# Graph layer on one core: row places read from SBUF as byte offsets, and two queues that each fetch a tile of every fourth group

## The chip, the cores and the metric

The kernel runs on one core of a Trainium2 chip. The metric is device microseconds (us) of one execution; the number quoted for a kernel is the median of several executions. Engines are called as the profile calls them: PE is TensorE (PEld its weight load), DVE is VectorE, ACT is ScalarE, POOL is GpSimd, SP is SyncE. A name with q behind it (ACTq, SPq) is the sequencer of that engine, which also issues DMAs.

## The reference

One pre-normalised graph layer over N = 12500 nodes with D = 256 features and E = 200000 edges, sorted by `dst`; H = 512.

```python
h = maximum(layernorm(x), 0)
agg = segment_sum(h[src], dst, num_segments=N)
z = (1 + eps_gin) * h + agg
t = relu(batchnorm(dot(z, W1) + b1, g1, bt1))
out = relu(batchnorm(dot(t, W2) + b2 + h, g2, bt2))
return x + out
```

The expensive part is `segment_sum(h[src], dst)`: 200000 rows have to be fetched from DRAM in the order of `src`, and rows with the same `dst` are added.

## The kernel before

**Tiles and groups.** 128 edges make a tile, 12 tiles (GT) a group; there are 1563 tiles (NTILE) and 131 groups (NG). For each tile the 128 rows named by `src` are brought into SBUF, one row to a partition. PE then multiplies them with a 0/1 matrix (`oh`, made by DVE at L600) that says which edge belongs to which of the next 128 nodes; all tiles of a group add up in one PSUM tile `ps` (L636). The group's sum is copied out (`zs`, L691 on DVE), moved to its place among the nodes by a second 0/1 matrix (`at`, L700; `pz`, L708), and added to `zc`, which holds 512 nodes at a time (L723). When all groups of a chunk of 512 nodes are in, PE multiplies it with W1 in four slices (`ph`, L733); DVE takes the slice's statistics (`st`, L744), ACT copies it to `ts` (L750) and stores it in DRAM (`t_tab`, L751). A group spans some 96 nodes, so a chunk has 5 1/3 groups and there are 0.75 slices to a group. `ph` has three PSUM buffers, `ts` four.

**Two halves of the edges.** For the first 30 groups (LEAD) the rows come from `x` itself and are normalised after they have arrived, while the normalised table `h_tab` (rows of 512 numbers, 2048 bytes: the value and its rounding rest) is still being written. From group 30 on, the rows come from `h_tab`.

**Who fetches the rows.** Nearly every tile is fetched by POOL with one indirect DMA of 128 rows (`gather`, L567), whose row numbers lie in SBUF (`srcT`). The table `SINGLES` (L31) takes single tiles away from POOL: tile 0 of the groups 34, 40, 46, ... is fetched by SP, tile 0 of the groups 37, 43, 49, ... by ACT, 15 tiles each. Such a tile is fetched row by row (`fetch`, L534 to L549): a piece is 32 rows; the engine loads the piece's 32 node numbers into registers (L541: first the address of `src` is loaded, then an offset added to it, then the 32 numbers loaded from DRAM), and then for each row multiplies the number by the row's size (an instruction that the trace calls FUSED_REGOPS) and issues one DMA of 2048 bytes (L546, after a MOVE). The four pieces of a tile are issued in steps of their own, from seven steps (SOONER) before the tile's group is added up to three steps before. The rows go to the twelve row places in `gta` and `gtb`, which the first 30 groups used before; each place has a semaphore, for which PE waits ahead of that tile's matmul. Tile 0 is the last one that PE takes in a group.

**Order of the work.** The program is written out by hand: each engine's instructions stand in the order of the Python loop over steps i, one step to a group. In step i POOL's gathers of group i + 4 (AHEAD) stand first, then the work of DVE and ACT (ACT: the copies `ts` with their stores, and now and then a scaling of `zc`, L593), then PE's sums of group i with the second matmul of group i - 3 and one slice of W1 between them, and last on SP the load of the next chunk of `zc` (L589) and on SP and ACT the pieces that are due. So on ACT a piece stands behind the copies of its step and ahead of those of the next.

**After the groups** (from about 1933 us) the chunks of `t` are read back, normalised, multiplied with W2, normalised again and added to `x`. The change does not touch this.

Of the kernel before, what the change touches and what calls it, by code (L numbers as in the profile page):

```python
# [7 lines left out]

F32 = mybir.dt.float32
F32R = mybir.dt.float32r  # L10
I32 = mybir.dt.int32
AF = mybir.ActivationFunctionType
OP = mybir.AluOpType
# [3 lines left out]
P = 128  # L17
R = 4
EPS = 1e-5
GT = 12  # L20
# [7 lines left out]
XIN = 1  # L28
PIECE = 32
SOONER = 7  # L30
SINGLES = (("sync", 34, 6), ("scalar", 37, 6))  # L31


COPIES = 2
# [6 lines left out]
def kernel(  # L41
# [16 lines left out]
    nc = tc.nc  # L58
    N, D = x.shape
# [29 lines left out]
    h_tab = dram.tile([N, 2 * D], F32, name="h_tab")  # L89
# [72 lines left out]
    at = 0  # L162
# [6 lines left out]
    with ExitStack() as es:  # L169
# [20 lines left out]
        at = 0  # L190
# [48 lines left out]
        place = raw.tile([P, NG], I32, name="place")  # L239
# [3 lines left out]
        for i in range(EARLY):  # L243
            for t in reversed(range(GT)):
                k = i * GT + t
# [21 lines left out]
        for k, (v, t0, rows, n, e) in enumerate(checks):  # L267
# [7 lines left out]
                op0=OP.add, op1=OP.max,  # L275
# [76 lines left out]
    def fast():  # L352

        parts = []
        for n0, w in chunks:
            n = w * R
# [20 lines left out]
        with ExitStack() as fs:  # L377
# [14 lines left out]
            with ExitStack() as es:  # L392
                rows_pool = es.enter_context(tc.tile_pool(name="rows", bufs=RING))
                sel = es.enter_context(tc.tile_pool(name="sel", bufs=2))
                zcp = es.enter_context(tc.tile_pool(name="zc", bufs=4))
                tsp = es.enter_context(tc.tile_pool(name="ts", bufs=4))
                ps_i = es.enter_context(tc.tile_pool(name="ps_i", bufs=1, space=PSUM))
# [82 lines left out]
                def h_chunk(g):  # L480
# [3 lines left out]
                    relus(((0, R, xts.pop(g)),), n, ((0, R, hts[g]),), "c", g)  # L484
                    nc.scalar.copy(both_place[:, :n, 0, :].bitcast(F32R), hts[g][:, :n, :])
                    x_chunk(g + 3)
# [34 lines left out]
                alone, due = {}, {}  # L521
                for name, i0, every in SINGLES:
                    for i in range(i0, NG - 8, every):
                        alone.setdefault(i, []).append((name, every))
                arrived = [tc.alloc_semaphore(f"arrived{k}") for k in range(len(singles_at))]
                placing = {}
                for i in sorted(alone):
# [6 lines left out]
                def fetch(name, step):  # L534

                    eng = getattr(nc, name)
                    for i, j, q in due.pop((name, step), ()):
                        k, _ = placing[i, j]
                        place, c = singles_at[k]
                        e0 = (i * GT + j) * P + q  # L540
                        _, ids = nc.values_load_multi_w_load_instructions(  # L541
                            src[e0 : e0 + PIECE].rearrange("(o e) -> o e", o=1), engines=[eng.engine],
                            min_val=0, max_val=N - 1, skip_runtime_bounds_check_because="src names nodes",
                        )
                        for r, node in enumerate(ids):
                            single = eng.dma_start(place[q + r : q + r + 1, c, :], h_tab[bass.ds(node, 1), :])  # L546
                            tc.no_tile_sem_insts.add(single.ins.name)
                            tc.add_to_no_dep_group(f"single{i}_{j}", single.ins)
                            single.then_inc(arrived[k], 16)  # L549
# [34 lines left out]
                zc, ohs, summed, zss, ats, placed, slices = {}, {}, {}, {}, {}, {}, {}  # L584
# [10 lines left out]
                def edges(i):  # L595
# [4 lines left out]
                    nc.vector.tensor_tensor(  # L600
                        oh.bitcast(F32R) if i >= LEAD else oh,
                        col[:, :P].unsqueeze(1).to_broadcast([P, n, P]),
# [186 lines left out]
                for c in range(NCH):  # L789
                    k = min(max(first(c) - 2, c + 2), NG - CLOSE - 1)  # L790
# [154 lines left out]
            with tc.tile_pool(name="ps_y", bufs=2, space=PSUM, reuse_waits="tile") as ps_y:  # L945
# [117 lines left out]
                for p in range(1, PAIRS - 1):  # L1063
                    a, b = 2 * p, 2 * p + 1
# [47 lines left out]
                a, b = 2 * p, 2 * p + 1  # L1112
# [45 lines left out]
            with tc.tile_pool(name="ps_o", bufs=4, space=PSUM, reuse_waits="tile") as ps_o:  # L1158
# [18 lines left out]
                for k, g in enumerate(order):  # L1177
# [15 lines left out]
                    for c0, c1, rows in pieces(g):  # L1193
                        if c0 == c1:
                            continue
                        if k == 0:
                            nc.vector.scalar_tensor_tensor(
                                xt[:rows, c0:c1, :], po[:rows, c0:c1, :], 0.0, xt[:rows, c0:c1, :],
                                op0=OP.max, op1=OP.add,
# [255 lines left out]
```

## Time and profile before

| what | value |
|---|---|
| median of 3 runs | 2136.57 us (2135.61 to 2137.64) |
| the profiled execution, its own time | 2139.61 us |
| span of its trace | 2137.7 us |
| POOL busy in the span | 1539.0 us, 72% |
| PE busy | 1470.1 us, 69% |
| DVE busy | 880.4 us, 41% |
| ACT busy | 490.3 us, 23% |
| time of the DMA packets, as a share of 16 engines' span | POOL's queue 56.6%, SP's 17.9%, ACT's 3.9% |

The busy times count what an engine computes; loading registers, register arithmetic and the issuing of DMAs do not count, so ACT with 23% can be occupied far more than that. In a line of groups stand the line of the program, the engine, the operation, the tiles, how many there are, the busy time, the mean of one in ns, and the idle time of the engine just ahead of them with what ended it; "issue" there means that the engine's own sequencer was the last to be ready.

### The profile page before, as it was taken

The page shows a single profiled execution, that of the slowest core. Times are in us where ns is not written, and L with a number is a line of the kernel's source. Part 1 is how long each engine was busy: PE and PEld are TensorE (multiplying, and loading weights), DVE is VectorE, ACT ScalarE, POOL GpSimd, SP SyncE. Part 2 cuts the span into 40 slices and gives each one's busy share as a digit, 9 for nine tenths or more (in the row PEclk, how much of TensorE's full clock was granted, in tenths as well). Part 3 has the DMA queues.
Part 4 walks back from the last instruction along what each step waited for, and adds up shares of the span by engine and source line. Part 5 has one row for each costly group of instructions (what it writes and reads, how often), then busy time and mean ns, then how long its engine had stood idle before and what let it go on. Part 6 is the DMA issues. An engine that isn't in the chain of part 4 may idle for free.

```text
span 2137.7 us, 25061 instructions
## 1 busy us (share of the span) xinstructions
PE 1470.1 (69%) x3698; PEld 822.5 (38%) x3698; DVE 880.4 (41%) x1296; ACT 490.3 (23%) x873; POOL 1539.0 (72%) x1579
## 2 busy tenths in 40 slices
PE   2656657675667776666666666766776666679997
PEld 2545445453333333333333333333333333335445
DVE  6666676653222232222223223223222222136997
ACT  4766677750000000000000000000000000004555
POOL 7777777777777777777777777777777777774640
PEclk9778888888776676766677677767677767679999
DMA  6777777658888778787877787877778787878888
GB/s 186 245 244 247 258 236 266 225 163 243 243 237 241 232 241 239 229 246 237 241 232 238 240 241 231 239 239 239 233 236 244 227 237 231 265 235 275 308 308 342
DMA packets 189893, 520.52 MB, mean 243 GB/s; under 512 B 34056, under 2 KB 49328, under 8 KB 189718
## 3 DMA queue, kind: packets, MB, share of 16 engines
q0 software_dynamic: 111088, 354.65, 56.6%
q1 hardware_dynamic: 59842, 134.01, 17.9%
q10 hardware_dynamic: 18788, 30.17, 3.9%
q14 instruction: 144, 1.18, 0.2%
q8 instruction: 31, 0.51, 0.1%
HBM read 441.90 MB, written 76.80 MB: 243 GB/s over the span
## 4 chain that ended last, share of the span: by engine, by line
POOL 46%; issue 19%; DMA 15%; PE 11%; DVE 5%; ACT 3%; SPq 0%; ACTq 0%; DVEq 0%; POOLq 0%
POOL gt L567 45%; DMA gt<-h_tab,srcT 7%; DMA gt<-in_x_dram,srcT 4%; DMA gta<-in_x_dram,srcT 3%; PE one L994 2%; PE ps L636 2%; PE pr L994 2%; PE pq L994 2%; PE ph L733 1%; DVE stc L434 1%; ACT gt L458 1%; DVE stg L434 1%; DVE zc L723 1%; DVE gt L512 1%; PE pz L708 1%
## 5 line engine op out<-in xcount | busy, mean ns | idle before, releaser
L567 POOL DMA_INDIRECT gt<-h_tab,srcT x1173 | 1108.8, 945 | 357.6 <-issue 345.4
L636 PE MATMUL ps<-gt,oh 128*128 128x512 f32 (+1 forms) x1590 | 821.4, 597 | 457.1 <-DMA gt<-h_tab,srcT 433.6
L636 PEld LDWEIGHTS ps<-gt,oh 128*128 128x128 f32 x1590 | 382.2, 241 | 873.3 <-DMA gt<-h_tab,srcT 685.3
L744 DVE BATCH_NORM_STATS2 st<-ph 128x6 f32<-128x512 f32 x96 | 66.8, 696 | 689.3 <-PE ph L733 689.3
L600 DVE TENSOR_TENSOR oh<-col,dstT 128x1536 fp32r<-128x1536 f32 (+1 forms) x129 | 226.3, 1755 | 240.6 <-PE ps L636 240.3
L750 ACT COPY ts<-ph 128x512 f32<-128x512 f32 x96 | 56.1, 584 | 1069.7 <-issue 760.6
L733 PE MATMUL ph<-zc,w1s 128*128 128x512 f32 (+1 forms) x392 | 260.8, 805 | 55.7 <-DVE gt L512 55.7
L567 POOL DMA_INDIRECT gt<-in_x_dram,srcT x216 | 212.3, 983 | 67.2 <-issue 28.3
L708 PE MATMUL pz<-at,zs 128*128 128x256 f32 x516 | 201.6, 533 | 17.8 <-DVE zc L723 10.9
L708 PEld LDWEIGHTS pz<-at,zs 128*128 128x128 f32 x516 | 141.9, 277 | 47.7 <-issue 10.9
L733 PEld LDWEIGHTS ph<-zc,w1s 128*128 128x128 f32 x392 | 103.1, 267 | 140.8 <-issue 74.7
L723 DVE TENSOR_TENSOR zc<-pz,zc 128x512 f32<-128x512 f32 (+7 forms) x185 | 90.8, 516 | 108.9 <-PE pz L708 108.9
L458 ACT ACTIVATE gt<-gt,nbg,rsg 128x256 f32<-128x256 f32 x216 | 108.1, 588 | 11.8 <-DVE nbg L452 11.8
L434 DVE BATCH_NORM_STATS2 stg<-gt 128x6 f32<-128x512 f32 x108 | 72.8, 695 | 88.3 <-DMA gt<-in_x_dram,srcT 88.1
L567 POOL DMA_INDIRECT gta<-in_x_dram,srcT x80 | 79.8, 997 | 24.4 <-issue 7.0
L500 PE MATMUL ph<-ident,gt 128*128 128x128 f32 x196 | 36.5, 332 | 87.1 <-DVE gt L512 70.2
L593 ACT ACTIVATE zc<-zc,gin 128x1024 f32<-128x1024 f32 (+1 forms) x25 | 28.2, 1128 | 291.4 <-issue 268.6
L691 DVE TENSOR_REDUCE zs<-ps 128x256 f32<-128x512 f32 x99 | 67.2, 679 | 19.0 <-PE ps L636 19.0
L636 PE MATMUL ps<-gta,oh 128*128 128x256 f32 (+1 forms) x232 | 69.6, 438 | 0.0
L500 PEld LDWEIGHTS ph<-ident,gt 128*128 128x128 f32 x196 | 27.0, 168 | 96.9 <-DVE gt L512 53.9
L1015 POOL TENSOR_TENSOR ax<-ax,by 128x1024 f32<-128x1024 f32 x10 | 25.4, 2536 | 51.0 <-ACT by L972 46.8
L700 DVE TENSOR_SCALAR at<-col,shift 128x256 f32<-128x256 f32 x129 | 61.1, 474 | 2.3 <-PE pz L708 2.3
(189 smaller groups left out, 1224.8 us busy)
## 6 DMA issues: line engine op xcount, KB each, us to landing
h_tab<-gt SPq DMA_DIRECT2D x24, 1024.0 KB
t_tab<-ts ACTq DMA_DIRECT2D x96, 256.0 KB
gta<-h_tab SPq DMA_DIRECT2D x1280, 2.0 KB
gta<-h_tab ACTq DMA_DIRECT2D x1280, 2.0 KB
gt<-h_tab,srcT POOLq DMA_INDIRECT x1173, 4.4
gt<-in_x_dram SPq DMA_DIRECT2D x24, 512.0 KB
h_cols<-gt SPq DMA_DIRECT2D x24, 512.0 KB
zc<-h_cols SPq DMA_DIRECT2D x24, 512.0 KB
```

What stands on the lines that cost most here:

```text
L434: nc.vector.bn_stats(st[:, c : c + 2, :].rearrange("p c s -> p (c s)"), two.rearrange("p c d -> p d c"),)
L458: nc.scalar.activation(slot(to, c), slot(v, c), AF.Relu, bias=nb[:, c : c + 1], scale=rs[:, c : c + 1])
L500: nc.tensor.transpose(ph[:, c * P : (c + 1) * P], ht[:, c, d * P : (d + 1) * P], ident)
L567: nc.gpsimd.indirect_dma_start(out=slot(ga, t - t0)[:rows], out_offset=None, in_=x if i < LEAD else h_tab, in_offset=bass.IndirectOffsetOn ...
L600: nc.vector.tensor_tensor(oh.bitcast(F32R) if i >= LEAD else oh, col[:, :P].unsqueeze(1).to_broadcast([P, n, P]), dstT[:, t0 : t0 + n].uns ...
L636: part = nc.tensor.matmul(to, lhsT=lhsT, rhs=rhs, start=(j == order[0]), stop=(j == order[-1]))
L691: nc.vector.tensor_reduce(zss[i], ps.rearrange("p k d -> p d k"), axis=mybir.AxisListType.X, op=OP.add)
L708: nc.tensor.matmul(pz[:, d, :n], lhsT=zs[:, d * P : (d + 1) * P], rhs=at[:, :n], start=True, stop=True)
L723: nc.vector.tensor_add(side, pz[:, :, a - lo : b - lo], side)
L733: nc.tensor.matmul(ph[:, :n], lhsT=w1s[:, d, f * P : (f + 1) * P], rhs=zc[c][:, d, :n], start=(d == 0), stop=(d == DC - 1),)
L744: nc.vector.bn_stats(st1[:, f, c, :], ph[:, :n])
L994: nc.tensor.matmul(ps, lhsT=w[:, k, :], rhs=t[:, k, :], start=(k == 0), stop=(k == DC - 1))
```

## The change

Three things change. The node numbers of the tiles in SINGLES are loaded once, near the start, into two small SBUF tiles (`nodes`, a row of 128 for each tile) by two DMAs on SP, and DVE multiplies each by the row's 2048 bytes (`starts`, one instruction for SP's tiles, one for ACT's). `fetch` loads its 32 registers from a row of `starts` instead of from DRAM. Since `h_tab` and the row place are named as bytes (`bitcast(U8)`), the register is the byte offset itself, and the multiplication for each row is gone from the program. And SINGLES now takes tile 0 of the groups 34, 38, ..., 122 for SP (23 tiles) and of the groups 36, 40, ..., 120 for ACT (22 tiles): 45 tiles instead of 30. A tile's four pieces now fall into four steps in a row, so that SP has one piece in each step from 27 to 118, and ACT one in each from 29 to 116.

```diff
--- before.py
+++ after.py
@@ -8,6 +8,7 @@
 
 F32 = mybir.dt.float32
 F32R = mybir.dt.float32r
+U8 = mybir.dt.uint8
 I32 = mybir.dt.int32
 AF = mybir.ActivationFunctionType
 OP = mybir.AluOpType
@@ -28,7 +29,7 @@
 XIN = 1
 PIECE = 32
 SOONER = 7
-SINGLES = (("sync", 34, 6), ("scalar", 37, 6))
+SINGLES = (("sync", 34, 4), ("scalar", 36, 4))
 
 
 COPIES = 2
@@ -392,6 +393,7 @@
             with ExitStack() as es:
                 rows_pool = es.enter_context(tc.tile_pool(name="rows", bufs=RING))
                 sel = es.enter_context(tc.tile_pool(name="sel", bufs=2))
+                lines = es.enter_context(tc.tile_pool(name="lines", bufs=1))
                 zcp = es.enter_context(tc.tile_pool(name="zc", bufs=4))
                 tsp = es.enter_context(tc.tile_pool(name="ts", bufs=4))
                 ps_i = es.enter_context(tc.tile_pool(name="ps_i", bufs=1, space=PSUM))
@@ -522,6 +524,20 @@
                 for name, i0, every in SINGLES:
                     for i in range(i0, NG - 8, every):
                         alone.setdefault(i, []).append((name, every))
+                ROW = 2 * D * 4
+                starts, line = {}, {}
+                for name, i0, every in SINGLES:
+                    mine = sorted(i for i in alone if (name, every) in alone[i])
+                    assert all(len(alone[i]) == 1 for i in mine)
+                    nodes = lines.tile([len(mine), P], I32, name="nodes_" + name)
+                    step = every * GT * P
+                    nc.sync.dma_start(
+                        nodes, bass.AP(tensor=src.tensor, offset=src.offset + i0 * GT * P, ap=[[step, len(mine)], [1, P]])
+                    )
+                    starts[name] = lines.tile([len(mine), P], I32, name="starts_" + name)
+                    nc.vector.tensor_scalar(starts[name], nodes, float(ROW), None, op0=OP.mult)
+                    line.update({i: k for k, i in enumerate(mine)})
+                h_bytes = h_tab.rearrange("n d -> (n d)").bitcast(U8)
                 arrived = [tc.alloc_semaphore(f"arrived{k}") for k in range(len(singles_at))]
                 placing = {}
                 for i in sorted(alone):
@@ -537,13 +553,16 @@
                     for i, j, q in due.pop((name, step), ()):
                         k, _ = placing[i, j]
                         place, c = singles_at[k]
-                        e0 = (i * GT + j) * P + q
-                        _, ids = nc.values_load_multi_w_load_instructions(
-                            src[e0 : e0 + PIECE].rearrange("(o e) -> o e", o=1), engines=[eng.engine],
-                            min_val=0, max_val=N - 1, skip_runtime_bounds_check_because="src names nodes",
-                        )
-                        for r, node in enumerate(ids):
-                            single = eng.dma_start(place[q + r : q + r + 1, c, :], h_tab[bass.ds(node, 1), :])
+                        k_line = line[i]
+                        _, ats = nc.values_load_multi_w_load_instructions(
+                            starts[name][k_line : k_line + 1, q : q + PIECE], engines=[eng.engine],
+                            min_val=0, max_val=(N - 1) * ROW, skip_runtime_bounds_check_because="src names nodes",
+                        )
+                        for r, at in enumerate(ats):
+                            single = eng.dma_start(
+                                place[q + r : q + r + 1, c, :].bitcast(U8),
+                                h_bytes[bass.ds(at, ROW)].rearrange("(o b) -> o b", o=1),
+                            )
                             tc.no_tile_sem_insts.add(single.ins.name)
                             tc.add_to_no_dep_group(f"single{i}_{j}", single.ins)
                             single.then_inc(arrived[k], 16)
```

POOL, the gathers from group 33 on (in step 29 and after), before; each row is one group, `gt_...` its buffer, the last number its gathers:

```order
L567 DMA gt_3133<-h_tab_60,srcT_70 128x512 x12
L567 DMA gt_3178<-h_tab_60,srcT_70 128x512 x11
L567 DMA gt_3412<-h_tab_60,srcT_70 128x512 x12
L567 DMA gt_3643<-h_tab_60,srcT_70 128x512 x12
L567 DMA gt_3683<-h_tab_60,srcT_70 128x512 x11
L567 DMA gt_3919<-h_tab_60,srcT_70 128x512 x12
```

and now:

```order
L586 DMA gt_3144<-h_tab_60,srcT_70 128x512 x12
L586 DMA gt_3383<-h_tab_60,srcT_70 128x512 x11
L586 DMA gt_3617<-h_tab_60,srcT_70 128x512 x12
L586 DMA gt_3848<-h_tab_60,srcT_70 128x512 x11
L586 DMA gt_4081<-h_tab_60,srcT_70 128x512 x12
L586 DMA gt_4318<-h_tab_60,srcT_70 128x512 x11
```

Every third group had 11 gathers, now every second; over the whole program 15 of the 1173 gathers from `h_tab` go, and 1158 stay.

ACT, in the middle of the groups, from the end of one piece to the first rows of the next, before (`gta1_81` is a row place, ISA is the multiplication of the node number):

```order
L546 DMA gta1_81<-h_tab_60 1x512
L750 COPY ts_6750<-ph_6528 128x512
L751 DMA t_tab_266<-ts_6750 128x512
L750 COPY ts_6794<-ph_6766 128x512
L751 DMA t_tab_266<-ts_6794 128x512
L541 TENSOR_LOAD in_src_dram_ptr
L541 REGISTER_ALU
L541 TENSOR_LOAD in_src_dram
L546 ISA
L546 DMA gta1_81<-h_tab_60 1x512
L546 ISA
```

and now, three pieces with the copies between them:

```order
L557 TENSOR_LOAD starts_scalar_313
L562 DMA gta1_81<-h_tab_60 1x2048 x32
L769 COPY ts_18520<-ph_18298 128x512
L770 DMA t_tab_266<-ts_18520 128x512
L557 TENSOR_LOAD starts_scalar_313
L562 DMA gta1_81<-h_tab_60 1x2048 x32
L557 TENSOR_LOAD starts_scalar_313
L562 DMA gta1_81<-h_tab_60 1x2048 x32
L612 ACTIVATE zc_18305<-zc_18305,gin1_84 128x1024
```

A piece was three loading instructions and 32 pairs of a multiplication and a DMA; it is one load and 32 DMAs, and there are more pieces. On SP a piece changes in the same way.

DVE, near the start, just ahead of the first `oh`, now (the two L538 rows are new, what stands around them stood there before):

```order
L146 TENSOR_TENSOR dstT_71<-dstT_71,col_300 128x1572
L425 TENSOR_SCALAR shift_72<-shift_72,row_303 128x131
L538 TENSOR_SCALAR starts_sync_309<-nodes_sync_307 23x128
L538 TENSOR_SCALAR starts_scalar_313<-nodes_scalar_311 22x128
L619 TENSOR_TENSOR oh_342<-col_300,dstT_71 128x1536
```

The two multiplications wait there for the two new DMAs, which stand on SP ahead of the first loads of `x`, and the first `oh` stands behind them.

## The prediction

> **What bounds the kernel now.** I read the page first: engines, chain, costliest groups. These rows of it matter, from its parts 1, 4 and 5:
>
> ```profile
> PE 1470.1 (69%) x3698; PEld 822.5 (38%) x3698; DVE 880.4 (41%) x1296; ACT 490.3 (23%) x873; POOL 1539.0 (72%) x1579
> ...
> POOL 46%; issue 19%; DMA 15%; PE 11%; DVE 5%; ACT 3%; SPq 0%; ACTq 0%; DVEq 0%; POOLq 0%
> ...
> L567 POOL DMA_INDIRECT gt<-h_tab,srcT x1173 | 1108.8, 945 | 357.6 <-issue 345.4
> ```
>
> POOL leads the chain, and its gathers cost 945 ns each plus an idle time of 357.6/1173 = 305 ns that ends in "issue": nothing else releases them. So POOL's period is (1108.8 + 357.6)/1173 = 1.250 us a gather. Next, the first and last gather in POOL's timeline, and the table of stretches (columns: stretch, length, then busy time of PE, PEld, DVE, ACT and POOL, granted clock, DMA share, GB/s):
>
> ```profile
> 3.19 1.10 POOL L246 DMA_INDIRECT gtb<-in_x_dram,srcF  x1 [0.94 <-DMA srcF<-in_src_dram]
> ...
> 1932.36 0.95 POOL L567 DMA_INDIRECT gt<-h_tab,srcT  x1 [0.30 <-issue]
> ```
>
> ```profile
> 520.00:1720.00 1200.00, 819.78 (x1594) 404.84 (x1594) 322.98 (x429) 54.91 (x79) 907.32 (x961) 0.71 0.80 237
> ```
>
> Between 3 and 1933 us POOL issues one gather behind another; in the 1200 us in the middle 961 of them, 1.249 us each. Who waits for whom in that stretch:
>
> ```profile
> ACT ts L750 <- issue: 701.4, 35, 23.1
> ...
> PE ps L636 <- DMA gt<-h_tab,srcT: 375.3, 481, 4.2
> ...
> ACT zc L593 <- issue: 268.6, 12, 40.3
> ```
>
> PE waits for gathers 375.3 us of the 1200. POOL is the bound; the 204 us behind 1933 are a tail that starts when the last gather is in. The two ACT rows are the warning: 970 us in which ACT computes nothing and is ended by its own sequencer. That is time spent loading registers and issuing rows; it comes back below.
>
> **What goes: 15 gathers.** 15 x 1.250 = 18.75 us of POOL. All of it is on the path, as POOL has no wait to give it back to. A group has 35/3 = 11.67 gathers before (14.58 us a step) and 11.5 now (14.38 us).
>
> **What comes to SP and ACT.** The rows of the fetch lines for ACT (smallest, median and largest ns), and the register load of `flag`, the one load from SBUF that the trace has:
>
> ```profile
> L546 ACTq FUSED_REGOPS  x1920: 37/37/43, 494.2 to 1778.0; - x192
> ...
> L546 ACTq MOVE gta<-h_tab x1280: 29/29/38, 494.4 to 1690.5; - x183
> L546 ACTq DMA_DIRECT2D gta<-h_tab x1280: 229/235/637, 494.4 to 1690.5; - x183
> ```
>
> ```profile
> L541 SPq TENSOR_LOAD <-in_src_dram x60: 3629/4766/7776, 445.0 to 1659.5; - x60
> L541 ACTq TENSOR_LOAD <-in_src_dram_ptr x60: 1045/1508/3995, 487.9 to 1757.5; - x60
> L541 ACTq ALU_OP  x60: 40/40/53, 489.5 to 1759.4; - x60
> L541 ACTq TENSOR_LOAD <-in_src_dram x60: 4263/4910/8126, 489.6 to 1759.4; - x60
> ```
>
> ```profile
> L1420 ACTq TENSOR_LOAD <-flag x1: 482/482/482, 25.6 to 25.6; - x1
> ```
>
> And one piece in ACT's timeline, then pieces of SP:
>
> ```profile
> 551.54 0.36 ACTq L751 DMA_DIRECT2D t_tab<-ts  x1
> 558.72 12.85 ACTq L546 DMA_DIRECT2D gta<-h_tab  x32
> 571.67 0.58 ACT L750 COPY ts<-ph 128x512 f32<-128x512 f32 x1 [20.16 <-issue]
> 572.28 0.36 ACTq L751 DMA_DIRECT2D t_tab<-ts  x1
> ...
> 594.08 1.15 ACT L593 ACTIVATE zc<-zc,gin 128x1024 f32<-128x1024 f32 x1 [20.75 <-issue]
> ```
>
> ```profile
> 835.45 13.36 SPq L546 DMA_DIRECT2D gta<-h_tab  x32
> ```
>
> ACT before: 6.82 us from the end of the store (551.90) to the first row's DMA, and 12.85 us for 32 rows, 19.67 us a piece; four pieces in six steps are 78.7 us. Copies: 0.75 a step, each 1.07 us with its store (571.57 to 572.64); `zc` 0.19 a step at 1.25. With them 84.9 us of 6 x 14.58 = 87.5: **ACT's sequencer is 97% taken before the change**, though only 5% busy by the row of the stretch. A quarter more rows would not have fitted.
>
> ACT now has one piece in each step. A row costs 12.85/32 = 402 ns. The three instructions add to 37 + 29 + 235 = 301, so some 34 ns lie ahead of each; without FUSED_REGOPS a row is 402 - 71 = 331 ns and 32 rows are 10.6 us. (I take MOVE as staying, and a DMA named in bytes as costing what one named in floats does: it is the same 2048 bytes.) With 0.80 of copies, 0.24 of `zc` and 0.1 at the seams: **11.7 us + L** of 14.38, where L is the load of 32 registers from SBUF, which the trace does not show.
>
> Bounds of L: not below the 0.48 us of one register from SBUF, not above the 4.91 us of 32 from DRAM. Between them two readings. If a load's time is mostly trips to memory, L scales as the short loads do: 4.91 x 0.48/1.51 = 1.6 us. If it is a cost of each register whatever the memory, (4.91 - 1.51)/30 = 0.113 us a register, and L = 0.48 + 31 x 0.113 = 4.0. I take 1.6: the DRAM loads run from 4.26 to 8.13 us with the same number of registers, so memory sets much of their time. Then ACT has 13.3 us of work in 14.38, 93%, less than before.
>
> How much L may be: ACT can fall behind for a while, since `ph` has three buffers and 0.75 slices are written a step, so PE first waits when ACT is about three steps late, 43 us. Over ACT's 88 pieces that allows 43/88 = 0.49 us a step. Full gain up to L = 14.38 + 0.49 - 11.7 = 3.2 us; all gain lost at 18.75/88 = 0.21 more, 3.4 us.
>
> SP: 13.36/32 = 418 ns a row, 347 without the multiplication, 11.1 us a piece; with L = 1.6 it is 12.7 of 14.38. SP has nothing else but a `zc` load every five steps, and its rows are issued four steps or more ahead of use.
>
> The Trainium skill speaks against this, in Runtime: NRT & Kernel Launch, section Instruction fetch mechanics: a register load takes about 200 ns for each register even in bulk, as each is a round trip. By it L would be 6.4 us, and the sum would come out above every bound taken here. The trace has 4.91 us for 32 from DRAM, 153 ns each, so the rule is too high by a third for DRAM, and no run here shows it for SBUF.
>
> **What else comes.** PE: a tile fetched by rows is multiplied without the faster type. From the groups by shape in the middle stretch:
>
> ```profile
> L636 PE MATMUL ps<-gt,oh 128*128 128x512 f32 x960 | 601.4, 674 | 380.3 <-DMA gt<-h_tab,srcT 375.3
> ...
> L636 PE MATMUL ps<-gta,oh 128*128 128x512 f32 x38 | 23.8, 714 | 0.0
> ```
>
> Such a tile leaves two records of 714 ns where a gathered one leaves one of 674, so each costs PE 0.75 us more; 15 of them are 11 us, against 375 us of waiting for gathers. Cost nothing; without that cover 11 us.
>
> Start: two small DMAs on SP ahead of `x`, and two multiplications on DVE that wait for them:
>
> ```profile
> 26.53 2.52 SPq L375 DMA_DIRECT2D gt<-in_x_dram  x4
> ...
> 29.12 3.41 DVE L600 TENSOR_TENSOR oh<-col,dstT 128x1536 f32<-128x1536 f32 x2
> ```
>
> SP issues them at 26.5 at some 0.6 us each (2.52/4), and DVE reaches them at 29.1; `oh` and the first `stg` stand behind. I allow 0 to 3 us of delay for DVE. POOL is then gathering groups that nobody holds up, so it costs nothing; without that cover 3 us.
>
> **The sum.** Against the profiled execution's own 2139.61 us (1.9 above its span): -18.75 + 0 + 0 = 2120.9. That execution is 3.0 us above the median of the runs, so against the median 2136.57: **2117.8 us**, 0.9% faster. Its own range is 2115 to 2121, from the spread of the runs (2 us) and the covers.
>
> **The rivals.**
>
> *ACT's sequencer becomes the bound* (slower). The register load costs as much for each register from SBUF as from DRAM. It decides from L = 3.4 us. For it: ACT is at 97% today, and the smallest load of 32 still takes 3.63 us (SP's row), so much of it may be fixed. Against: one value from SBUF takes a third of the short load from DRAM. At L = 4.0 a step of ACT is 15.7: 1.32 x 88 = 116, less the 43 of slack, less 18.75, is +54: 2191 us. If SBUF were no quicker than DRAM, L = 4.91: 2.23 x 88 - 43 - 18.75 = +134: 2271. Chance 0.21, 0.13 of it up to 2191. (The skill's rule above is this rival at its far end: 3.7 x 88 - 43 - 18.75 would give +264, 2401 us; 0.02 of the 0.21 is for that.)
>
> *L between 3.2 and 3.4*: the gain partly eaten, 2118 to 2137 us. Chance 0.04, half of it within 0.2%.
>
> *The rows crowd the DMA engines* (slower). 32 rows on two queues in 14.38 us are 4.45 rows a us, against 256/87.5 = 2.93 before. Queue and landing rows from the DMA view, 1000 to 1100 us, then landing of gathers from 1800 to 1860, when no rows are fetched:
>
> ```profile
> q0 software_dynamic: 6469, 21.21, 72.4%
> q10 hardware_dynamic: 1121, 1.81, 5.0%
> q1 hardware_dynamic: 458, 0.85, 2.5%
> ...
> gt<-h_tab,srcT POOLq DMA_INDIRECT x81, 4.4
> ```
>
> ```profile
> gt<-h_tab,srcT POOLq DMA_INDIRECT x49, 4.4
> ```
>
> ACT's queue moves 1.81 MB in 5.0% of 1600 us, 22.6 GB/s on an engine, 91 ns a row. Spread over 16 engines that is 2.5%, nothing. On one engine it would be 40%, on top of 72% for gathers and some 7% for the other two queues: 119%, and 106% before. As 106% went without a sign, with gathers landing in 4.4 us with and without rows, the shares overstate; if 106% was just the limit, a step would be 1.19/1.06 x 14.38 = 16.1 us, and 88 x 1.8 - 18.75 = +140: 2277 us. Chance 0.04. [...]
>
> *It doesn't do what it says*: POOL ends earlier, but the tail waits for something else that ends when it did. Behind 1933 us all work hangs on the last sums, so little speaks for it: 2136.6, chance 0.03.
>
> **How the numbers follow.** The forecast has 0.68. A measurement of this kernel can tell about 0.2% (4.3 us) from no change. Faster: 0.68 + 0.02 = 0.70; within 0.2%: 0.02 + 0.03 = 0.05; slower: 0.21 + 0.04 = 0.25. The range begins at 2115, the low end of the forecast, and has to reach into the slower cases: up to 2191, the price of L = 4.0, it holds 0.68 + 0.04 + 0.03 + 0.13 = 0.88; without the price of that reading it would hold 0.75.
>
> **What would show it.** Right: 1158 gathers from `h_tab`, still at 945 + 305 ns, the last one near 1913.6; PE still waiting for gathers; a load of `starts` of 1 to 2 us; rows at 330 ns without FUSED_REGOPS; ACT now waiting for PE or DVE, where before it was ended by its own sequencer. Wrong: a load above 3.2 us with ACT still ended by issue throughout and PE waiting for `ts` or for rows instead of for gathers; POOL with waits of more than 0.3 us; or gathers that land later than 4.4 us while rows are in flight.

## The result, and the profile after

| | before | after |
|---|---|---|
| median of 4 runs each | 2136.92 us (2135.61 to 2137.64) | 2159.92 us (2159.05 to 2160.25) |
| ratio, 95% interval | | 1.0108 (1.009 to 1.0125) |
| profiled execution, its span | 2139.61, 2137.7 us | 2159.82, 2158.0 us |
| gathers from `h_tab` | 1173 | 1158 |
| POOL's last gather starts at | 1932.36 us | 1953.24 us |

The kernel became slower by 23 us where 19 us of gain were forecast. A second measurement of the same program gave 2157.5 against 2137.07 us, 1.0091 (1.0062 to 1.012).

The page of the changed kernel, parts 4 and 5: the chain by engine, and the costliest group.

```profile
ACTq 51%; issue 13%; PE 9%; DMA 8%; ACT 7%; DVE 5%; POOL 5%; SPq 0%; DVEq 0%; POOLq 0%
...
L586 POOL DMA_INDIRECT gt<-h_tab,srcT x1158 | 1095.3, 946 | 393.4 <-issue 348.3
```

POOL led the chain with 46% before; now it is at 5%, and ACT's sequencer at 51%, of which 40% stand at the rows (L562) and 10% at the loads (L557). The gathers cost what they did (946 ns), and 15 of them are gone, but POOL now has idle time that is not its own: 393.4 - 348.3 = 45 us, against 12 before. The waits in the middle stretch, 520 to 1720 us:

```profile
ACT ts L769 <- issue: 741.8, 50, 16.8
...
ACT zc L612 <- issue: 269.5, 14, 30.6
...
PE ph L752 <- ACT ts L769: 245.2, 27, 25.0
...
PE ps L655 <- DMA gt<-h_tab,srcT: 147.5, 224, 1.5
...
PE ps L655 <- DMA gta<-h_tab: 87.8, 7, 31.9
...
PE ps L655 <- DMA gtb<-h_tab: 55.5, 3, 31.9
```

PE waits for gathers 147.5 us, where it waited 375.3; in exchange it waits 245.2 us for ACT to copy `ph` to `ts`, in 27 long pieces, and 143 us for tiles fetched row by row (the two last rows). In the trace all of the latter are ACT's tiles; PE never waits for one of SP's. ACT, for its part, is still ended by its own sequencer. So which part of ACT's step is longer than forecast? The rows of the new load (smallest, median, largest ns, then first and last start), and some 60 us of ACT's timeline, where "x32" is one piece:

```profile
L557 SPq TENSOR_LOAD <-starts_sync x92: 2061/2175/3021, 440.7 to 1748.3; - x92
L557 ACTq TENSOR_LOAD <-starts_scalar x88: 2168/2719/3203, 478.0 to 1825.9; - x88
```

```profile
814.00 11.36 ACTq L562 DMA_DIRECT2D gtb<-h_tab  x32
825.45 0.59 ACT L769 COPY ts<-ph 128x512 f32<-128x512 f32 x1 [14.70 <-issue]
826.07 0.36 ACTq L770 DMA_DIRECT2D t_tab<-ts  x1
829.53 12.17 ACTq L562 DMA_DIRECT2D gtb<-h_tab  x32
841.80 1.15 ACT L612 ACTIVATE zc<-zc,gin 128x1024 f32<-128x1024 f32 x1 [15.77 <-issue]
844.12 12.16 ACTq L562 DMA_DIRECT2D gta<-h_tab  x32
856.38 0.59 ACT L769 COPY ts<-ph 128x512 f32<-128x512 f32 x1 [13.43 <-issue]
856.99 0.36 ACTq L770 DMA_DIRECT2D t_tab<-ts  x1
860.41 12.43 ACTq L562 DMA_DIRECT2D gta<-h_tab  x32
```

A load takes 2.72 us, and 32 rows take 11.4 to 12.4 us, 373 ns a row on average between 520 and 1720 us, where the sum had 10.6 us. From the first load at 478.0 to the last at 1825.9 there are 87 pieces: **15.49 us a piece**, against the 14.38 of a step. ACT falls behind by 1.1 us with each piece. PE begins to wait for `ts` and for ACT's tiles between 900 and 1000 us, when ACT is 30 to 37 us late by that. Until about 1300 us POOL does not notice: it issues 80 or 81 gathers in each 100 us, as before. From there to 1800 us it issues 73 to 76, and there the time goes.

One more view changed, the time from a gather's issue to its landing in the same stretch (smallest, median, largest us). The row of before, then that of after:

```profile
DMA to landing us min/median/max: 3.5/4.4/8.1
```

```profile
DMA to landing us min/median/max: 6.0/6.9/10.7
```

So two theories stood. *ACT's order*: ACT's sequencer works through loads, rows and copies one after another, and these are simply more than 14.38 us. *Crowding*: the rows of both queues and the gathers hold each other up in the DMA engines, and ACT only shows it. In the trace's records of the rows, the stall has a shape: at ACT a row's DMA takes 237 to 247 ns on average from the second to the sixth us after a load, and 377 to 400 ns from the eleventh to the thirteenth; before, it took 234 to 238 ns throughout. 18% of ACT's and 19% of SP's rows between 520 and 1720 us took over 300 ns, where 3% and 0% did before (the 3% are the first row of each of ACT's pieces, which takes over 300 ns in both kernels). MOVE stayed at 29 ns. It looks like a queue that fills up during a piece and drains during the next load; no view shows such a queue itself.

### The profile page after: what moved, and what is told of

Its sections match the earlier page's. It is cut to its first block, busy times and chain, and to the rows that moved or that the text cites. A ratio compares the mean times of both kernels' runs of the same rounds, so it can differ in the third digit from the quotient of the medians.

```text
span 2158.0 us, 24906 instructions
## 1 busy us (share of the span) xinstructions
PE 1288.5 (60%) x3713; PEld 779.2 (36%) x3713; DVE 878.5 (41%) x1298; ACT 490.5 (23%) x873; POOL 1525.7 (71%) x1564
## 4 chain that ended last, share of the span: by engine, by line
ACTq 51%; issue 13%; PE 9%; DMA 8%; ACT 7%; DVE 5%; POOL 5%; SPq 0%; DVEq 0%; POOLq 0%
ACTq L562 40%; ACTq L557 10%; POOL gt L586 5%; DMA gt<-in_x_dram,srcT 4%; DMA gta<-in_x_dram,srcT 3%; PE one L1013 2%; ACT ts L769 2%; ACT gt L460 2%; PE pr L1013 2%; PE pq L1013 2%; PE ph L752 1%; PE ps L655 1%; DVE stc L436 1%; ACTq L770 1%; ACT zc L612 1%
## 5 line engine op out<-in xcount | busy, mean ns | idle before, releaser
L586 POOL DMA_INDIRECT gt<-h_tab,srcT x1158 | 1095.3, 946 | 393.4 <-issue 348.3
L655 PE MATMUL ps<-gt,oh 128*128 128x512 f32 (+1 forms) x1575 | 650.7, 525 | 189.2 <-DMA gt<-h_tab,srcT 168.4
L655 PEld LDWEIGHTS ps<-gt,oh 128*128 128x128 f32 x1575 | 353.0, 225 | 456.5 <-DMA gt<-h_tab,srcT 290.1
L752 PE MATMUL ph<-zc,w1s 128*128 128x512 f32 (+1 forms) x392 | 273.0, 838 | 348.9 <-ACT ts L769 296.0
L752 PEld LDWEIGHTS ph<-zc,w1s 128*128 128x128 f32 x392 | 96.8, 260 | 444.0 <-ACT ts L769 309.4
L727 PE MATMUL pz<-at,zs 128*128 128x256 f32 x516 | 162.3, 446 | 18.5 <-DVE zc L742 11.0
L655 PE MATMUL ps<-gta,oh 128*128 128x256 f32 (+1 forms) x254 | 89.9, 489 | 120.6 <-DMA gta<-h_tab 120.6
L727 PEld LDWEIGHTS pz<-at,zs 128*128 128x128 f32 x516 | 117.2, 229 | 43.3 <-issue 11.0
L460 ACT ACTIVATE gt<-gt,nbg,rsg 128x256 f32<-128x256 f32 x216 | 108.1, 587 | 11.4 <-DVE nbg L454 11.4
L655 PEld LDWEIGHTS ps<-gta,oh 128*128 128x128 f32 x254 | 52.5, 211 | 135.1 <-DMA gta<-h_tab 124.5
L655 PE MATMUL ps<-gtb,oh 128*128 128x256 f32 (+1 forms) x124 | 50.8, 555 | 71.9 <-DMA gtb<-h_tab 56.0
```

The source lines that it names most:

```text
L460: nc.scalar.activation(slot(to, c), slot(v, c), AF.Relu, bias=nb[:, c : c + 1], scale=rs[:, c : c + 1])
L586: nc.gpsimd.indirect_dma_start(out=slot(ga, t - t0)[:rows], out_offset=None, in_=x if i < LEAD else h_tab, in_offset=bass.IndirectOffsetOn ...
L655: part = nc.tensor.matmul(to, lhsT=lhsT, rhs=rhs, start=(j == order[0]), stop=(j == order[-1]))
L727: nc.tensor.matmul(pz[:, d, :n], lhsT=zs[:, d * P : (d + 1) * P], rhs=at[:, :n], start=True, stop=True)
L752: nc.tensor.matmul(ph[:, :n], lhsT=w1s[:, d, f * P : (f + 1) * P], rhs=zc[c][:, d, :n], start=(d == 0), stop=(d == DC - 1),)
```

## The experiments

Three expectations count the tiles fetched by rows wrongly (61, 73 and 75): there were 30 before, 45 in the changed kernel, 36 with every fifth group, and 38 with SyncE every fourth and ScalarE every sixth. The gathers that they build on are right, but with SyncE every fourth and ScalarE every sixth there are 8 fewer than before, where two expectations have 7.

**Half the gathers.** Between group 34 and group NG-9 every second gather is left out; the sums take the neighbouring tile's rows instead, so this kernel computes something else.

```diff
+                def twin(i, j):
+                    return j - 1 if 34 <= i < NG - 8 and j >= 2 and j % 2 == 0 else j
...
+                        if twin(i, t - t0) != t - t0:
+                            continue
...
-                        lhsT, rhs, to = oh[:rows, j, :], slot(ga, j)[:rows], ps
+                        lhsT, rhs, to = oh[:rows, j, :], slot(ga, twin(i, j))[:rows], ps
```

> The changed kernel with nearly half of GpSimd's gathers left out between group 34 and group NG-9 (the sums use the neighbouring tile's rows in their place, so the output isn't the reference's); the one-row instructions, their loads and their cadence stay. If it is the gathers in flight that make a row dearer to issue than 331 ns and a load longer than 1.6 us, rows fall back to about 325 to 335 ns with fewer than 5% of them above 300 ns, a step of ScalarE to 13.5 to 14.2 us, and the whole to 2020 to 2060 us where the kernel before takes 2137. If the rows of the two queues hold each other up without the gathers, rows stay near 378 ns, the step at 15.4 to 15.8 and the time at 2130 to 2160. Where the kernel before takes some 3100 us, the first theory says that the 0.7 us stalls shrink with the gathers, to below 2700; the second says above 2950.

Measured: one run of 2049.0 us. ACT's loads and pieces in it:

```profile
L557 ACTq TENSOR_LOAD <-starts_scalar x88: 2155/2564/3666, 477.3 to 1729.6; - x88
```

```profile
812.17 11.11 ACTq L562 DMA_DIRECT2D gtb<-h_tab  x32
823.38 1.15 ACT L617 ACTIVATE zc<-zc,gin 128x1024 f32<-128x1024 f32 x1 [14.21 <-issue]
825.70 10.81 ACTq L562 DMA_DIRECT2D gta<-h_tab  x32
```

The rows fell to 247 ns a DMA (from 281 in the same stretch), with 5% above 300 ns instead of 18%, and a piece now takes (1729.6 - 477.3)/87 = 14.39 us, a little more than was expected of the gathers' theory. With the same rows and fewer gathers the stalls are all but gone: the gathers are needed to make a row dear. Note the second number: 11.7 + 2.7 = 14.4 us is just what the prediction's sum gives for ACT with the measured load. Without the stalls, by that sum, the load alone would have been inside the allowance (full gain up to 3.2 us). With so few gathers POOL is idle in between, and ACT's sequencer heads the chain with 49% at that 14.4 us.

**Fewer rows.** Two kernels change only the table:

```diff
-SINGLES = (("sync", 34, 4), ("scalar", 36, 4))
+SINGLES = (("sync", 34, 5), ("scalar", 36, 5))
```

> A tile every fifth group on both engines, places from SBUF. If ScalarE's sequencer alone cost the gain, its 4 pieces now have 5 steps of 14.4 us (4 x 14.9 + 5 x 0.8 = 64 of 72 us), it is free, and POOL's 6 gathers fewer than in the kernel before decide: 2129 (2127 to 2132). If rows in flight delay the gathers whatever ScalarE does, the late gathers eat the gain: 2134 to 2145. Where the kernel before takes some 3100 us it is 2860 as twice before.

```diff
-SINGLES = (("sync", 34, 4), ("scalar", 36, 4))
+SINGLES = (("sync", 34, 4), ("scalar", 37, 6))
```

> SyncE every fourth group, ScalarE every sixth, places from SBUF: 75 tiles. ScalarE alone theory: 7 gathers fewer than before, 2127 (2125 to 2130), since SyncE's step is 10.7 + 2.2 + its other DMAs = some 13.5 us. If SyncE's rows with the gathers fill its DMA engine, as ScalarE's do, PE comes to wait for SyncE's tiles or POOL for late gathers: 2137 or above. Where the kernel before takes some 3100 us it is 3055 as twice before.

Measured: 2130.89 us for every fifth group, 0.9969 (0.9957 to 0.998) of the kernel before; 2127.73 us for SyncE every fourth and ScalarE every sixth, 0.9957 (0.994 to 0.9973). Both are faster than either kernel, and by what the missing gathers are worth: 6 x 1.250 = 7.5 us forecast and 6.3 measured, 8 x 1.250 = 10.0 and 9.4 (against 2137.15). The second one's chain, its waits in the middle stretch, and then ACT's timeline with a full piece:

```profile
POOL 44%; DMA 19%; issue 18%; PE 10%; DVE 5%; ACT 3%; SPq 0%; ACTq 0%; DVEq 0%; POOLq 0%
```

```profile
ACT ts L769 <- DVE st L763: 731.2, 47, 28.6
...
PE ps L655 <- DMA gt<-h_tab,srcT: 369.0, 523, 2.9
```

```profile
822.05 10.54 ACTq L562 DMA_DIRECT2D gtb<-h_tab  x32
832.68 0.59 ACT L769 COPY ts<-ph 128x512 f32<-128x512 f32 x1 [14.05 <-issue]
```

This is the picture that the prediction had asked of the change: POOL leads, PE waits for gathers, ACT waits for DVE, 32 rows in 10.54 us. SyncE is the telling engine. It issues just the rows that it issues in the changed kernel, a piece in each step, and here 0% of them took over 300 ns; there 19% did. SyncE's rows got dear only when ScalarE's came more often. The two queues share something, and that something has a limit between these two cadences.

**The places from SBUF alone**, with the cadence of before:

```diff
-SINGLES = (("sync", 34, 4), ("scalar", 36, 4))
+SINGLES = (("sync", 34, 6), ("scalar", 37, 6))
```

> Only the places from SBUF, with the cadence of before (every sixth group on both): the same gathers as before, ScalarE with more room. If POOL's gathers set the step, no change: 2135 to 2139. If rows that come faster (about 331 ns instead of 402) delay the gathers, slower: 2140 or more. Where the kernel before takes some 3100 us it is 2740 as twice before.

Measured: 2139.66 us, 1.0008 (0.9998 to 1.0017): no difference, with 3% and 1% of the rows above 300 ns. That covers the two loads and two multiplications at the start as well: they cost nothing that shows. Gathers landed in 5.4 us instead of 4.4 and nothing came of it, so a late gather alone is no loss here.

**Shorter rows.** Each single row is cut to its first 256 bytes, then to its first 1024; the rest is not fetched, and the output lacks it.

```diff
-                                place[q + r : q + r + 1, c, :].bitcast(U8),
-                                h_bytes[bass.ds(at, ROW)].rearrange("(o b) -> o b", o=1),
+                                place[q + r : q + r + 1, c, :].bitcast(U8)[:, :256],
+                                h_bytes[bass.ds(at, 256)].rearrange("(o b) -> o b", o=1),
```

> The changed kernel with each single row cut to its first 256 bytes, an eighth. The run with half the gathers brought rows back to 235 to 246 ns; what is open is whether the rows crowd the gathers by their bytes or by their number. By bytes: rows at 228 to 245 ns, ScalarE's step 14.2, time 2117 to 2130. By number (each row also has a packet of its own for the semaphore): rows at 270 to 280 ns, time 2150 to 2162. Where the kernel before takes some 3100 us, near 3020 as twice before.

> The changed kernel with each single row cut to its first 1024 bytes, a half. With 256 bytes rows were at 232 to 245 ns and the gathers landed in 8.4 us, later than in the changed kernel. If the number of rows is what delays gathers, they land in 6.9 to 8.5 us again and the time is 2150 to 2190. If it is bytes, and the 256-byte rows had a cost of their own, rows stay at 228 to 250 ns, gathers land in 4.5 to 6.2 us and the time is 2117 to 2130.

Measured: 2185.2 us with 256 bytes, 1.0231 (1.0209 to 1.0254); 2129.45 us with 1024 bytes, 0.9958 (0.9944 to 0.9972). Neither expectation holds as it stood. Rows above 300 ns at ACT fall with their bytes, 18%, 11%, 4% for 2048, 1024 and 256, so bytes matter to the rows' stall although the number of rows is the same. With 1024 a piece of ACT takes (1791.2 - 477.1)/87 = 15.10 us, and the gain is back in part, although the gathers land later than ever:

```profile
DMA to landing us min/median/max: 6.6/8.3/10.5
```

With 256 they land as late, and here POOL itself waits for earlier gathers (waits of POOL, middle stretch):

```profile
POOL gt L586 <- issue: 252.1, 797, 2.9
POOL gt L586 <- DMA gt<-h_tab,srcT: 85.8, 107, 3.4
```

With 1024 bytes that second row is 21.8 us, so an eighth of a row hurts in a way of its own that a half does not. The Trainium skill (DMA: Bandwidth & Descriptors, section Specifications) says that below 512 bytes an engine reads, changes and writes back; the two runs agree with that, and show no more of it than the 85.8 us.

**The copies on VectorE.** The copy of `ph` to `ts` leaves ACT, its store stays.

```diff
-                def take(c, f, copy=nc.scalar.copy):
+                def take(c, f, copy=nc.vector.tensor_copy):
```

> The changed kernel with the copy of ph to ts made by VectorE instead of ScalarE (the store of ts stays on ScalarE's queue). ScalarE's step loses the 0.6 us of the copy in its order, and TensorE no longer waits for ScalarE before ph is free again. If ScalarE's sequencer is what sets the step (15.4 to 15.8 us against 14.4 of the gathers), the step falls to about 14.9 and the time to 2110 to 2140, faster than the kernel before. If the gathers or SyncE's rows set it, it stays at 2155 to 2165. Where the kernel before takes some 3100 us the 0.7 us stalls rule and this comes out within 1% of 3040.

Measured: 2147.57 us, 1.0046 (1.0033 to 1.006). It gains 12 us on the changed kernel, which lies between the two ranges expected, and the reason is in the load's row:

```profile
L557 ACTq TENSOR_LOAD <-starts_scalar x88: 2140/2752/3204, 477.6 to 1822.9; - x88
```

(1822.9 - 477.6)/87 = 15.46 us a piece: ACT got no faster, although 0.75 x 0.6 us of its step were gone. Its rows took 294 ns instead of 281, 0.4 us a piece, and used it up. So ACT's order alone does not set the pace; what was freed there the rows took back. PE no longer waits behind ACT's rows for the copy, but it now waits 355 us for the tiles that ACT fetches, where it waited 143 us:

```profile
PE ps L655 <- DMA gta<-h_tab: 230.9, 9, 41.1
...
PE ps L655 <- DMA gtb<-h_tab: 124.4, 5, 38.4
```

ACT is late with its pieces as before, and PE meets that at another place.

**ACT's load twice.** A first kernel loaded the places a second time without using them, and the program held 88 loads at ACT as before: it is the changed kernel once more, at 2157.97 us, and tells nothing of the load. A second one uses half of each load:

```diff
+                        if name == "scalar":
+                            _, again = nc.values_load_multi_w_load_instructions(
+                                starts[name][k_line : k_line + 1, q : q + PIECE], engines=[eng.engine],
+                                min_val=0, max_val=(N - 1) * ROW, skip_runtime_bounds_check_because="src names nodes",
+                            )
+                            ats = ats[: PIECE // 2] + again[PIECE // 2 :]
```

> The changed kernel in which ScalarE reads the places of each of its 88 pieces twice. If ScalarE's serial order is what turns loads and rows into time, its step grows from 15.5 by 2.7 less what the rows recover (up to 1.5): 16.7 to 18.2, and over 87 steps the time grows by 100 to 235 us, to 2260 to 2395. If the DMA engines set the step and ScalarE only waits for them, the second load replaces stalls and the time stays within 2150 to 2190.

> The changed kernel in which ScalarE loads the 32 places of each of its 88 pieces twice and uses the first 16 of one load and the last 16 of the other, so that 176 loads stand in the program. If ScalarE's serial order turns loads and rows into time, its step grows from 15.5 by 2.7 less what the rows recover in the longer step (up to 1.5): 16.7 to 18.2 us, and over 87 steps the whole by 100 to 235, to 2260 to 2395. If the DMA engines set the step and ScalarE only waits for them, the load takes the place of stalls: 2150 to 2190.

The second took 3231.98 us beside 3117.1 us of the kernel before, on a chip as in the next paragraph, where the changed kernel itself was not run. ACT's sequencer heads its chain with 47%. What a dearer load costs is left open by this.

**Nine runs that can't be set beside the rest.** On three occasions, the last being that run, the kernel before itself took 3044 to 3133 us, on chips where MOVE and row DMA alike can stop for some 0.7 us: in the first trace taken there, every sixth group, a quarter of SP's MOVEs did, which else take 29 ns. Eight of those runs are the same kernels as above:

> The new fetch (offsets in SBUF, rows named in bytes) with the old table: tiles of every sixth group, 30 tiles, 1173 gathers. Sequencer theory (ACT's own loading and issuing is the bound of the changed kernel): ACT needs (4/6) x (10.6 + 2.7) + 1.0 = 9.9 us of a step of 14.58, so POOL bounds, and the time is that of the kernel before, 2135 to 2139 us; PE waits for gathers as before. Crowding theory (the rows' bytes on one DMA engine are the bound): the mean rate of rows is that of the kernel before, so the same time, but since the two engines rest between pieces, gathers land later while both issue and not otherwise. Rival: the new form of fetch is itself dear (a DMA named in bytes, or registers read from SBUF): then slower than 2142 us with the old table too.

> The changed kernel, with each single row fetched as its first 256 bytes instead of 2048 (the rest of those 45 tiles is left out and old contents are multiplied); the number of loads, DMAs and waits is the same. Crowding theory: with an eighth of the bytes the issue of a row falls back from some 380 ns to 331, gathers land in 4.4 us instead of 6.9, ACT needs 10.6 + 2.7 + 1.1 = 14.4 of 14.38 us, so the gain comes: 2117 to 2124 us. Sequencer theory with a limit on the number of DMAs: rows stay at 380 ns and the time at 2155 to 2162 us.

> The changed kernel with tiles of every fifth group on both engines: 36 tiles, 6 gathers fewer than before. Sequencer theory: ACT needs 0.8 x (12.1 + 2.7) + 1.0 = 12.9 of 14.45 us, POOL bounds, 6 x 1.25 = 7.5 us below before: 2129 us (2127 to 2132). Crowding theory: 3.6 rows a us instead of 4.4 and 2.9; if that is too many for one engine, gathers land late and the time is 2137 or more.

> The changed kernel with SP at every fourth group and ACT at every sixth (37, 43, ...): 38 tiles, 8 gathers fewer than before. Sequencer theory: ACT is far from its limit (10 of 14.5 us a step) and SP, which nobody waits for soon, needs 32 x 0.36 + 2.2 = 13.7: POOL bounds, 10 us below before: 2127 us (2125 to 2130). Crowding theory: 3.7 rows a us; if that is too many, rows on SP are issued at 400 ns or more, gathers land late and the time is 2137 or more.

> Places as byte offsets from SBUF, but the old cadence (every sixth group on each of SyncE and ScalarE, 61 tiles, as before). POOL then has the gathers of before, which set 14.58 us a step, and ScalarE is far from its limit (4 pieces in 6 steps of 17 us instead of 19.7). Both theories (ScalarE's sequencer sets the step; or the number of one-row transfers in flight slows the gathers) expect no change where the kernel before takes 2137 us: 2135 to 2139. If the kernel before again takes some 3100 us, the stalls of the one-row instructions rule, and this kernel falls well below it.

> The changed kernel, each single row cut to its first 256 bytes, an eighth (the rest of the row is not fetched). If what slows the issue of the rows and the landing of the gathers is bytes on the DMA engines, rows go back to about 331 ns each, ScalarE's step to about 14.3 us and the time to 2117 to 2124. If it is the number of one-row instructions and their offsets (their writing of descriptors), rows stay near 378 ns and the time near 2155 to 2162.

> The changed kernel with a tile every fifth group on both engines: 73 tiles, 9 gathers fewer than every fourth would save beyond. If ScalarE's sequencer sets the step of the changed kernel, its 4 pieces now lie in 5 steps: (15.9 - 0.8) x 0.8 + 0.8 = 12.9 us of 14.4, so it is free again and POOL's gathers decide: about 6 gathers fewer than before, 2129 (2127 to 2132). If a row costs more with every further row in flight, less of it comes: 2133 to 2150.

> SyncE every fourth group (as changed), ScalarE every sixth (as before). If only ScalarE's step is too long, this gains what POOL's gathers say: some 7 fewer, 2127 (2125 to 2130). If SyncE's sequencer or the DMA engines are at their limit with every fourth as well, it stays at 2137 or above.

| kernel | first time, and its ratio | second time, and its ratio |
|---|---|---|
| every sixth | 2742.62, 0.8942 (0.8779 to 0.9105) | 2745.11, 0.8821 (0.8731 to 0.8911) |
| every fifth | 2862.46, 0.9337 (0.9188 to 0.9487) | 2858.88, 0.9195 (0.9122 to 0.9268) |
| SyncE fourth, ScalarE sixth | 3055.18, 0.9949 (0.9898 to 1.0) | 3059.73, 0.9853 (0.9777 to 0.9928) |
| 256 bytes a row | 3019.07, 0.9862 (0.9644 to 1.0079) | 3025.15, 0.974 (0.9667 to 0.9814) |

There the time goes roughly with the number of row instructions that SP has to issue: 1920 rows of two instructions in the first line, 2304 in the second, 2944 in the last two, and 1920 rows of three in the kernel before. It does not do so exactly: the kernel before has 5760 of them and is slower than the last two with 5888. The order of the cadences is thus turned round, and nothing was concluded from these runs for the others. The changed kernel has no run on such a chip; its second measurement comes from one like the first:

> The changed kernel itself, unaltered, to have it beside the kernel before on the chip of the experiments. Where the kernel before takes about 2137 us it takes 2160. Where the kernel before takes some 3100 us, what counts is the number of instructions that SyncE's sequencer goes through for single rows (5760 before, with three a row, 5888 now, with two a row): then about 3040 (3000 to 3080), that is, no slower than before, and a step of ScalarE that is too long would not show.

It took 2157.5 us, as told at the top.

## Why the prediction was wrong

- **Right: what a gather is worth.** 1.250 us each, all of it on the path. The two kernels with 6 and 8 gathers fewer gained 6.3 and 9.4 us.
- **Right: covers.** PE's dearer matmuls and DVE's start cost nothing that shows: the kernels that gained have the first, and the places from SBUF alone have the second.
- **Mis-sized: L.** 1.6 us was taken, 2.7 came at ACT, 2.2 at SP. The bounds held it, and at 2.7 the sum still forecasts the gain. A load of 32 from SBUF is neither a matter of trips alone (1.6) nor of registers alone (4.0). From the Trainium skill's 200 ns a register (Runtime: NRT & Kernel Launch, section Instruction fetch mechanics) an estimate of L would be 6.4 us; the row has 2719/32 = 85 ns, and the measurement decides.
- **The step that failed: "without FUSED_REGOPS a row is 402 - 71 = 331 ns".** The arithmetic is right, and with fewer rows or fewer gathers it comes near the truth: 32 rows in 10.54 us are 329 ns with ScalarE every sixth group, and 338 ns a row was the mean with half the gathers. But it takes a row's price at a rate of 2.93 rows a us and uses it at 4.45. In the changed kernel, which came to 4.26 rows a us, a row was 373 ns at ACT, 1.3 us a piece more. 11.7 + 2.7 + 1.3 is 15.7, measured 15.49. With the measured step, the prediction's own formula gives 88 x 1.11 - 43 - 18.75 = +36 us, 2172.5 us from the median 2136.57; 2159.92 was measured, which fits an allowance of some 56 us in place of the 43. PE did wait from 30 to 37 us of lateness on, and POOL's pace fell at about 59.
- **It took both.** By the same sum neither the load nor the stalls alone would have cost the gain: 11.7 + 2.7 = 14.4 us and 11.7 + 1.6 + 1.3 = 14.6 us both lie within 14.38 + 0.49. No run separates them, and the copies on VectorE, where the rows took back what was freed, speak against counting on the second.
- **The rival that it was.** The warning was rightly put on ACT's sequencer, which heads the chain as that rival said, but its cause, a load above 3.4 us, did not occur. The cause is that of the rival with a chance of 0.04, rows that crowd the DMA engines. Its reckoning for one engine, rows on top of 72% for gathers and 7% for other queues (72 + 7 + 9.1 for each row a us) orders the runs with whole rows well: some 95% with half the gathers (47% of their own), with 2 to 5% of the rows over 300 ns, 106% before, 111 for every fifth, 113 for SyncE fourth and ScalarE sixth, all with 0 to 3%, and 119% in the changed kernel (118 at its measured 4.26 rows a us), with 18 to 19%. This is a reckoning; no view gives the share of a single engine, and the 7% hold 1.7% of the rows themselves, which it so counts twice. What spoke against it in the prediction, that 106% went without a sign, was true, and no argument against 119%. Its price of 2277 us was too high, since it took 106% for the limit, and by the same reckoning the limit lies above 113.

What is left open is the thing that the two queues share. In the records of the row packets those of one queue never overlap in time and those of the two queues do (28% begin before the other's has ended), which is not what one engine that takes one packet at a time would show. The Trainium skill (DMA: Bandwidth & Descriptors, section Why a DMA increments its semaphore by 16 and not by 1) states that a DMA issued from SP or ACT that uses k engines runs on the lowest-numbered k of them. The records have one data packet for each row (2630 of 2048 bytes for SP's 2656 rows between 520 and 1720 us); if that means k = 1, the rows of both queues share one engine. That both queues stall together, and only together with the gathers, agrees with it. Rows spread over several engines would tell, and were not tried. Nor does the reckoning explain all: a row packet of 1024 bytes took 56 ns on average, so it would be 72 + 7 + 4.45 x 5.6 = 104% there, and 11% of the rows still took over 300 ns.

## What to carry to other kernels

When a change raises the rate of small transfers, do not take an issue time measured at the old rate as given (331 ns here became 373): look in the trace whether issue times grow towards the end of a burst, and raise the rate in steps. Here a cadence one notch lower (SyncE every fourth group, ScalarE every sixth) turned +1.1% into -0.4%, without any other edit. And freeing time on the engine that issues the rows did not speed it up here: of 0.44 us freed in a piece the rows took back 0.4.

## What the runs showed that was not expected

- Gathers landed in a median of 4.4 us at 2.9 rows a us, 5.4 with the same rows in quicker bursts, 6.3 and 6.1 at 3.5 and 3.8, 6.9 in the changed kernel, 7.0 in it with half the gathers, 8.3 with half rows; the kernel with 8.3 gained 0.4% all the same, with 21.8 us of POOL's waits for earlier gathers. A later landing by itself cost little in these runs.
- A load of 32 registers from SBUF took 2.2 us at SP and 2.7 us at ACT, the same instruction.
- Single rows cut to 256 bytes made POOL wait 85.8 us for earlier gathers, rows cut to 1024 bytes 21.8.
